# Loading, turning and masking the first batch of an attention and graph-attention kernel in another order

## The chip, the cores and the metric

The kernel runs on one core of a Trainium2 chip. The metric is the device time of one execution in microseconds (us), as the median of repeated runs. Engines are named as in the profile: PE is TensorE (matmul; PEld its weight loads), DVE is VectorE, ACT is ScalarE, POOL is GpSimd, SP is SyncE, which here only issues loads and stores.

## The reference

x is 8 x 2048 x 256, adj is 2048 x 2048. Two layers, each followed by a residual and a layer norm. Layer 0 is attention with 4 heads of 64, in which the softmax is taken separately in each of 8 chunks of 256 keys and the 8 results are added. Layer 1 is graph attention with additive scores.

```python
# layer 0
q, k, v = x @ Wq.T + bq, x @ Wk.T + bk, x @ Wv.T + bv        # then split into heads
scores = clip(q . k / 8, -10, 10)                            # (b, h, n, chunk, key in chunk)
attn = softmax(where(mask == 0, -10, scores))                # over the keys of one chunk
ctx = einsum('bhnjc,bhjcd->bhnd', attn, vc)                  # summed over chunks
y = layernorm(ctx @ Wo.T + bo + x) * gamma + beta
x1 = layernorm(x + y)
# layer 1
Wh = (x1 @ W).reshape(B, N, 4, 64)
e = leaky_relu(s_src[i] + s_dst[j], 0.2), -inf where adj == 0
h = elu(softmax(e, over j) @ Wh)
out = layernorm(x1 + h)
```

## The kernel before

The work goes batch by batch, eight times. Everything on each engine runs in the order in which the program text issues it.

**The head.** `project(b, g)` makes the five steps of group g (512 of the 2048 nodes; four groups): `load` fetches x, `turn` brings features onto the partitions (`xT`), then come keys, values and queries, which are matmuls against `wk_sb` (L315), `wv_sb` (L331) and `wq_sb` (L315) with an evacuation by ACT each (L323, L338). Here `load` is `load_turned`: eight DMAs (L269) of 64 KB in pieces of 32 floats, laid out so that one 32 x 32 block transpose on DVE (L281, `turned`) finishes the turn. For batch 0 this runs alone, before any attention.

**The masks.** `Masks` cuts adj into 48 pieces: 16 tiles of 128 rows times three banks of 6, 5 and 5 column tiles. Each call of `masks.step()` first sends pending stores, then loads one piece (`araw`, L214), turns an earlier one (`turn`: bf16 transposes on PE into `pm`, L236, then DVE writes `clip`, L238, and ACT writes `edge`, L240) and makes the 0/1 bits `ab` of another (L226). The stores go to `clipD`, one table for each quarter of the queries, and `edgeD`, one for each bank. Seventeen steps lie between the pieces of the head; the others are taken one per slot in batch 0.

**Constants.** `finish_constants` folds `a_src` and `a_dst` into `w1_sb` (`wa`, L167 and L168 on DVE), multiplies the value bias through the output weights (L178 on PE) and corrects `bo_sb` and `beta_sb`. It is called after the head. Its `wa` tiles share two buffers with `clip`.

**Slots.** A batch of attention is 64 slots: four query chunks (`q`), two head pairs, eight key chunks, so 16 slots (`i`) for each query chunk. A slot computes the scores of the next slot on PE (L371, `ps`), clips and masks them on DVE against an int8 `slab` loaded from `clipD` (L382, `pr`), exponentiates on ACT (L394) and multiplies by the values on PE (`product`, L406); POOL normalizes and adds up. The work on the chunk finished before (`Between`: output projection L521, two norms, then x1 stored to DRAM and loaded again turned as `x1t`) is spread over slots by the tables AHEAD, BESIDE, BEHIND and AFTER: x1t is loaded in slot 12, DVE turns it in slot 14 (`turn`, L281, `x1T`), and its four layer-1 projections (`values`, L565, `pw`) stand at the ends of slots 14, 15, 0 and 1. In the first chunk's slots there is no such group yet. In slot 61 the first load of the next batch's x is issued, and in slot 63 it is turned on DVE.

**Between batches** an explicit list (`order`) interleaves the last chunk's work with the next batch's keys, values and queries. From batch 1 on, the slots also carry layer 1 of the batch before (L702 on DVE, L722 on PE).

PSUM for projections, scores and wide outputs comes from two tiles of two banks used in turn (`two_banks`); `psM` is one bank, `psL` two.

Of the kernel before, what the change touches and what calls it, by code (L numbers as in the profile page):

```python
# [22 lines left out]
def adj_resnorm_kernel(  # L23
# [19 lines left out]
    nc = tc.nc  # L43
    B, N, F = x.shape
    H, D = a_src.shape
    NT = N // P
    NCH = N // CH
# [8 lines left out]
    QT = CH // P  # L56
    CLIP = 10.0 * 8.0
    FAR = 100.0
    BANKS = (6, 5, 5)
# [139 lines left out]
    class Masks:  # L199
# [1 line left out]


        def __init__(self):
            self.pieces = [(t, m) for t in range(NT) for m in range(len(BANKS))]
            self.raw, self.bits, self.done = [], [], []
            self.next = 0

# [50 lines left out]
    def load_x(b, g, name):  # L258
        t = blocks.tile([P, QT, F], F32, tag="xb", name=name)
        nc.sync.dma_start(out=t, in_=by_node(x, b, g))  # L260
        return t
# [12 lines left out]
    def load_turned(dram, b, g, name):  # L274
        t = blocks.tile([P, KC, CH], F32, tag="xb", name=name)
        load_squares(t, dram[b, g * CH : (g + 1) * CH, :])
        return t

    def turned(t, name):
        dst = blocks.tile([P, KC, CH], F32, tag="xT", name=name)  # L280
        nc.vector.transpose(dst.rearrange("p c n -> p (c n)"), t.rearrange("p c n -> p (c n)"))  # L281
        return dst

    def transposed(src, name):

        dst = blocks.tile([P, KC, CH], F32, tag="xT", name=name)
        pt = two_banks([P, KC, CH], "pt")
        for c in range(KC):
            for k in range(QT):
                nc.tensor.transpose(  # L290
                    pt[:, c, k * P : (k + 1) * P], src[:, k, c * P : (c + 1) * P], identf
                )
        nc.scalar.copy(dst, pt)
        return dst

    def project(b, g):

        cols = slice(g * CH, (g + 1) * CH)
        st = {}

        def load():
            st["x"] = load_turned(x, b, g, "xp")

        def turn():
            st["xT"] = turned(st["x"], "xT")

        def linear(dst, w, bias, apart=False):
            if apart:
                pps = [psL.tile([P, CH], F32, tag="psL", name="pp") for _ in range(KC)]
            else:  # L310
                pp = two_banks([P, KC, CH], "pp")
                pps = [pp[:, c, :] for c in range(KC)]
            for c in range(KC):
                for kc in range(KC):
                    nc.tensor.matmul(  # L315
                        pps[c],
                        lhsT=w[:, kc, c * P : (c + 1) * P],
                        rhs=st["xT"][:, kc, :],
                        start=(kc == 0),
                        stop=(kc == KC - 1),  # L320
                    )
            for c in range(KC):
                nc.scalar.activation(  # L323
                    dst[:, c, cols], pps[c], AF.Identity, bias=bias[:, c : c + 1]
                )

        def values():
            pv = two_banks([P, QT, F], "pv")
            for u in range(QT):
                for kc in range(KC):  # L330
                    nc.tensor.matmul(  # L331
                        pv[:, u, :],
                        lhsT=st["xT"][:, kc, u * P : (u + 1) * P],
                        rhs=wv_sb[:, kc, :],
                        start=(kc == 0),
                        stop=(kc == KC - 1),
                    )
            nc.scalar.copy(  # L338
                vaug[:, QT * g : QT * (g + 1), :, :D],
                pv.rearrange("p t (h d) -> p t h d", h=H),  # L340
            )

        return [
            load,
            turn,
            lambda: linear(kT, wk_sb, bk_sb),
            values,
            lambda: linear(qT, wq_sb, bq_sb, b > 0 and g == NCH - 1),
        ]
# [145 lines left out]
    class Between:  # L495
# [88 lines left out]
    BESIDE = {  # L584
        1: [lambda o: o.bias()],
        4: [lambda o: o.add((0, 1))],
        5: [lambda o: o.add((2, 3)), lambda o: o.a.stats((0, 1))],
        6: [lambda o: o.a.stats((2, 3)), lambda o: o.shift()],
        8: [lambda o: o.scale()],
        9: [lambda o: o.again(), lambda o: o.b2.stats((0, 1))],  # L590
        10: [lambda o: o.b2.stats((2, 3))],
        14: [lambda o: o.turn()],
# [6 lines left out]
        14: lambda o: o.values((0,)),  # L599
        15: lambda o: o.values((1,)),  # L600
    }
    AFTER = {0: lambda o: o.values((2,)), 1: lambda o: o.values((3,))}

    def factors(b, sd, waug):
# [203 lines left out]

    masks = Masks()
    groups = [project(0, g) for g in range(NCH)]  # L810
    groups[0][0]()
    for _ in range(2):
        masks.step()
    groups[1][0]()
    for g in range(NCH):
        for k, piece in enumerate(groups[g][1:]):
            if k == 1 and 0 < g < NCH - 1:
                groups[g + 1][0]()
            piece()
            if g or k:  # L820
                masks.step()
    finish_constants()

# [41 lines left out]
    for b in range(B):  # L867
# [12 lines left out]
        if closing:  # L880
            closing.do(-1)
        group = None
        for s in range(SLOTS):
            q, hp, c = where[s]
            i = s % QS
            send()
            if s + 3 < SLOTS:
                load_slab(s + 3)
            if i == 0:
                before = group  # L890
                group = Between(b, q - 1, sd, waug) if q else None
            if i == 1 and q:
                load_context(b, q - 1, 1)
            if i == QS // 2 + 1:
                load_context(b, q, 0)
            if group and i in AHEAD:
                AHEAD[i](group)
            if s == SLOTS - 3 and b + 1 < B:
                turns = [project(b + 1, g) for g in range(NCH)]
                turns[0].pop(0)()  # L900
            if s:
                normalize(s - 1)
            if s + 1 < SLOTS:
                scores(s + 1)

            if s == SLOTS - 1 and b + 1 < B:
                turns[0].pop(0)()
            if i == 3 and q:
                turn_context(q - 1, 1)
            if i == QS // 2 + 3:  # L910
                turn_context(q, 0)
            if group:
                for step in BESIDE.get(i, ()):
                    step(group)
            elif closing:
                closing.do(s, behind=False)
            product(s, 0, not lower)
            if s + 1 < SLOTS:
                for u in range(KT):
                    exps(s + 1, u)  # L920
            if lower:
                if b + 1 < B or s < SLOTS - LATE:
                    lower.step()
            elif masks.left():
                masks.step()
            product(s, 1, not lower)

            if before and i in AFTER:
                AFTER[i](before)
            if i == 0 and q:  # L930
                send_context(b, q - 1, 1)
            if i == QS // 2:
                send_context(b, q, 0)
            if group and i in BEHIND:
                BEHIND[i](group)
            elif closing and not q:
                closing.do(s, beside=False)
        normalize(SLOTS - 1)
# [2 lines left out]
        before = group  # L941
        gd, fs = factors(b, sd, waug)
        group = None
# [21 lines left out]
        if b + 1 < B:  # L965
            (k0, v0, q0), (l1, t1, k1, v1, q1), (l2, t2, k2, v2, q2), (l3, t3, k3, v3, q3) = turns
            rest = [lambda: lower.rest(1)] if lower else []
            order = [begin, *rest, l1, *rest, lambda: before.values((2, 3)), *rest, ctx, *rest, k0]
            order += [steps[0], t1, steps[1], v0, steps[2], steps[3], l2, k1, steps[4], q0]
            order += [steps[5], v1, t2, l3, steps[6], q1, steps[7], k2, steps[8], steps[9], t3, v2]  # L970
            order += [lambda: [load_slab(s) for s in range(3)], fs[0], q2, fs[1], k3, fs[2], v3]
            order += [lambda: scores(0), q3, lambda: [exps(0, u) for u in range(KT)]]
        else:

            step = lower.step
            order = [begin, lambda: before.values((2, 3)), steps[0], step, ctx, step, steps[1], step]
            order += [steps[2], step, steps[3], step, steps[4], step, steps[5], step, steps[6], step]
            order += [steps[7], step, steps[8], step, steps[9], step, fs[0], step, fs[1], step, fs[2]]
            order += [step, lambda: lower.rest(4)]
            assert sum(p is step for p in order) == LATE  # L980
# [61 lines left out]
```

## Time and profile before

| | us |
|---|---|
| median of 7 runs (range) | 3843.93 (3842.74 to 3847.5) |
| the profiled execution, device time | 3843.94 |
| its span, first to last instruction | 3842.1 |
| PE busy | 3685.4 (96%) |
| DVE busy | 3204.3 (83%) |
| ACT busy | 1948.2 (51%) |
| POOL busy | 1385.4 (36%) |
| first matmul starts | 17.77 |
| last projection of the head ends | about 74.3 |
| first masked scores of slot 0 on DVE | 80.99 |
| keys of batch 1 start | 408.29 |

The granted TensorE clock of the execution is 0.993 of full speed. Matmuls are pipelined and their ends are modelled, so a busy PE is not PE at its peak. Durations are read from one profiled execution, and starts are counted from the start of its span.

### The profile page before, as it was taken

To read this page: it belongs to the slowest core of one execution; us is meant where nothing else is said; L and a number is where in the kernel's file an instruction comes from. 1 tells how busy PE (TensorE), PEld (TensorE's weight loads), DVE (VectorE), ACT (ScalarE), POOL (GpSimd) and SP (SyncE) were. 2 spreads that over 40 slices of the span, in tenths; PEclk is the share of its full clock that TensorE was granted. 3 is DMA by queue.
4 is the path that set the end of the run, shared out by engine and by line. 5 is a ranking of instruction groups with operands and counts; after the bars stand their busy time and mean duration, and the time that the engine had idled before them with its cause. 6 is when DMAs were issued, how large, how long until landed. Compare 5 with 4: busy or idle time off the path is not lost. (4 is left out here: it accounts for less than half of the span.)

```text
span 3842.1 us, 160215 instructions
## 1 busy us (share of the span) xinstructions
PE 3685.4 (96%) x72068; PEld 2745.0 (71%) x72068; DVE 3204.3 (83%) x4810; ACT 1948.2 (51%) x3601; POOL 1385.4 (36%) x1202
## 2 busy tenths in 40 slices
PE   6999999999999999999999999999999999999787
PEld 4656677776777777776777767777677777776676
DVE  3876499986999779995999959998699977998798
ACT  3666445554555555554555545555455555555321
POOL 0444233342343333433443324343343333334310
PEclk9999999999999999999999999999999999999999
DMA  7642333333443343333433334333343433333354
GB/s 149 155 110 62 84 94 99 97 92 100 112 103 99 82 122 103 100 97 82 135 94 100 99 89 136 97 98 88 106 112 97 103 83 116 106 100 85 93 149 123
DMA packets 771328, 398.48 MB, mean 104 GB/s; under 512 B 442576, under 2 KB 735824, under 8 KB 770640
## 3 DMA queue, kind: packets, MB, share of 16 engines
q1 hardware_dynamic: 720640, 354.54, 36.6%
q10 hardware_dynamic: 50000, 33.70, 2.7%
q8 instruction: 563, 9.22, 1.0%
q14 instruction: 125, 1.02, 0.1%
HBM read 331.22 MB, written 56.89 MB: 101 GB/s over the span
## 5 line engine op out<-in xcount | busy, mean ns | idle before, releaser
L382 DVE SCALAR_TENSOR_TENSOR pr<-ps,slab 128x1024 f32<-128x1024 f32 x1024 | 1192.7, 1206 | 213.5 <-PE ps L371 210.8
L702 DVE SCALAR_TENSOR_TENSOR e<-srow,gd,et 128x640 f32<-128x640 f32 (+1 forms) x1536 | 1349.6, 935 | 9.9 <-PE pa L722 5.4
L406 PEld LDWEIGHTS pc<-vaug,pr 128*64 128x64 f32 x32768 | 1040.6, 138 | 440.3 <-issue 257.5
L406 PE MATMUL pc<-vaug,pr 128*64 128x65 f32 x32768 | 1158.2, 224 | 38.8 <-ACT raw L413 31.0
L394 ACT ACTIVATE pr<-pr 128x1024 f32<-128x1024 f32 x1024 | 1049.2, 1057 | 151.3 <-DVE pr L382 137.5
L722 PE MATMUL pa<-waug,e 128*64 128x65 f32 x32768 | 1081.4, 224 | 42.6 <-DVE e L702 40.0
L722 PEld LDWEIGHTS pa<-waug,e 128*64 128x64 f32 x32768 | 1020.0, 139 | 68.2 <-DVE e L702 41.0
L371 PE MATMUL ps<-qT,kT 64*128 64x512 f32 x4096 | 1026.8, 618 | 6.9 <-DVE pr L382 6.6
L428 POOL TENSOR_TENSOR part<-raw,rd 128x512 f32<-128x512 f32 x448 | 468.7, 1046 | 1464.6 <-DVE rd L421 1452.1
L413 ACT COPY raw<-pc 128x260 f32<-128x260 f32 x1024 | 385.0, 377 | 1193.6 <-PE pc L406 1149.6
L371 PEld LDWEIGHTS ps<-qT,kT 64*128 64x128 f32 x4096 | 351.1, 186 | 331.8 <-issue 204.4
L430 POOL TENSOR_TENSOR acc<-acc,part 128x512 f32<-128x512 f32 x448 | 574.1, 1281 | 35.2
L421 DVE RECIPROCAL rd<-raw 128x8 f32<-128x8 f32 x512 | 101.2, 198 | 118.7 <-ACT raw L413 115.2
L428 POOL TENSOR_TENSOR acc<-raw,rd 128x512 f32<-128x512 f32 x64 | 66.7, 1043 | 347.2 <-DVE rd L421 346.4
L750 ACT ACTIVATE hh<-pa,dn 128x64 f32<-128x64 f32 x512 | 114.5, 320 | 100.7 <-DVE dn L746 100.7
L565 PE MATMUL pw<-w_sb,x1T 128*128 128x264 f32 x512 | 138.4, 406 | 7.8 <-DVE x1T L281 7.8
L315 PE MATMUL pp<-xT,wk_sb 128*128 128x512 f32 x256 | 120.1, 613 | 26.4 <-DVE xT L281 19.8
L481 POOL TENSOR_TENSOR rs_c<-rs_c,nhalf 128x4 f32<-128x4 f32 x32 | 55.6, 1737 | 228.7 <-DVE off_c L480 228.7
L521 PE MATMUL po<-wo_sb,qT 128*128 128x256 f32 x512 | 125.5, 390 | 2.1 <-DVE qT L448 1.5
L281 DVE STREAM_TRANSPOSE xT<-xp 128x1024 f32<-128x1024 f32 x32 | 39.6, 1239 | 105.0 <-PE pw L565 67.0
L315 PE MATMUL pp<-xT,wq_sb 128*128 128x512 f32 x256 | 116.1, 596 | 0.0
L331 PE MATMUL pv<-wv_sb,xT 128*128 128x256 f32 x512 | 115.9, 380 | 0.0
(90 smaller groups left out, 1896.6 us busy)
## 6 DMA issues: line engine op xcount, KB each, us to landing
et<-edgeD SPq DMA_DIRECT2D x256, 320.0 KB, 3.2
slab<-clipD SPq DMA_DIRECT2D x512, 128.0 KB, 3.5
et<-edgeD SPq DMA_DIRECT2D x128, 384.0 KB, 3.4
srow<-rowD SPq DMA_DIRECT2D x64, 320.0 KB, 4.3
xp<-in_x_dram SPq DMA_DIRECT2D x256, 64.0 KB, 2.3
xg<-in_x_dram SPq DMA_DIRECT2D x32, 512.0 KB, 4.7
x1D<-y ACTq DMA_DIRECT2D x32, 512.0 KB, 3.1
x1g<-x1D SPq DMA_DIRECT2D x32, 512.0 KB, 5.7
```

Source lines behind the costliest of these rows:

```text
L315: nc.tensor.matmul(pps[c], lhsT=w[:, kc, c * P : (c + 1) * P], rhs=st["xT"][:, kc, :], start=(kc == 0), stop=(kc == KC - 1),)
L371: nc.tensor.matmul(ps[:, k, :], lhsT=kT[rows, hp, t * P : (t + 1) * P], rhs=qT[rows, hp, cols], start=True, stop=True,)
L382: nc.vector.scalar_tensor_tensor(pr, pss[u], -CLIP, slab[:, u, :].unsqueeze(1).to_broadcast([P, 2, CH]), op0=ALU.max, op1=ALU.min,)
L394: nc.scalar.activation(pr, pr, AF.Exp, scale=0.125)
L406: nc.tensor.matmul(pc[z * D : (z + 1) * D, i, :], lhsT=probs[s][u][:, k, i * P + z * D : i * P + (z + 1) * D], rhs=vaug[:, KT * c + u, 2 * ...
L413: nc.scalar.copy(raws[s][:, k], pc)
L428: nc.gpsimd.tensor_mul(part, raw[:, :, :, :D], rd.to_broadcast([P, 2, QT, D]))
L430: nc.gpsimd.tensor_add(accv, accv, part)
L521: nc.tensor.matmul(po[:, k, :], lhsT=qT[:, c, t * P : (t + 1) * P], rhs=wo_sb[:, c, :], start=(c == 0), stop=(c == KC - 1),)
L565: nc.tensor.matmul(pw[:, k, : F + 2 * H], lhsT=self.x1T[:, c, u * P : (u + 1) * P], rhs=w1_sb[:, c, :], start=(c == 0), stop=(c == KC - 1),)
L702: nc.vector.scalar_tensor_tensor(e[:, :w], self.rows[n][:, :w], self.gd[:, h, j : j + 1], self.edge[k // JG][:, j % JG, :w], op0=ALU.max, ...
L722: nc.tensor.matmul(self.pa[z * D : (z + 1) * D, i * D1 : (i + 1) * D1], lhsT=e[:, i * P + z * D : i * P + (z + 1) * D], rhs=self.waug[:, j ...
```

## The change

It touches the head and batch 0 only.

- The 48 mask pieces are taken quarter by quarter and, inside a quarter, bank by bank, where before each row tile went through its three banks. Sizes and number stay.
- In batch 0, x is loaded with one plain DMA for each group (`load_x`) and turned by eight fp32 transposes on PE into a two-bank PSUM tile, which DVE copies to `xT`. Later batches keep the eight strided loads and the block transpose.
- The head's order is written out: loads of groups 0 and 1 first, two mask steps, the turn of group 0; then for each group keys, step, values, step, turn of the next group, load of the one after, queries, step. That is fourteen mask steps in the head; the remaining ones are in slots.
- `finish_constants` is called after the queries of group 1.
- In batch 0, x1's turn moves from slot 14 to 15, and its four projections from the ends of slots 14, 15, 0, 1 to those of 15, 0, 1, 2. For the last chunk the second of them goes into the list between batches.

```diff
@@ class Masks
-            self.pieces = [(t, m) for t in range(NT) for m in range(len(BANKS))]
+            self.pieces = [
+                (QT * q + u, m) for q in range(NCH) for m in range(len(BANKS)) for u in range(QT)
+            ]
@@ transposed, project
-    def transposed(src, name):
+    def transposed(src, name, copy=nc.scalar.copy):
...
-        nc.scalar.copy(dst, pt)
+        copy(dst, pt)
...
         def load():
-            st["x"] = load_turned(x, b, g, "xp")
+            st["x"] = load_turned(x, b, g, "xp") if b else load_x(b, g, "xp")
 
         def turn():
-            st["xT"] = turned(st["x"], "xT")
+            if b:
+                st["xT"] = turned(st["x"], "xT")
+            else:
+                st["xT"] = transposed(st["x"], "xT", nc.vector.tensor_copy)
@@ tables of the slots
+    BESIDE_0 = {i: steps for i, steps in BESIDE.items() if i != 14} | {15: BESIDE[14]}
+    BEHIND_0 = {i: step for i, step in BEHIND.items() if i != 14} | {15: BEHIND[14]}
+    AFTER_0 = {i: lambda o, i=i: o.values((i + 1,)) for i in range(3)}
@@ the head
     groups[0][0]()
+    groups[1][0]()
     for _ in range(2):
         masks.step()
-    groups[1][0]()
+    groups[0][1]()
     for g in range(NCH):
-        for k, piece in enumerate(groups[g][1:]):
-            if k == 1 and 0 < g < NCH - 1:
-                groups[g + 1][0]()
-            piece()
-            if g or k:
-                masks.step()
-    finish_constants()
+        _, _, keys, values, queries = groups[g]
+        keys()
+        masks.step()
+        values()
+        masks.step()
+        if g + 1 < NCH:
+            groups[g + 1][1]()
+        if g + 2 < NCH:
+            groups[g + 2][0]()
+        queries()
+        masks.step()
+        if g == 1:
+            finish_constants()
@@ the slots
+        beside, behind, after = (BESIDE, BEHIND, AFTER) if b else (BESIDE_0, BEHIND_0, AFTER_0)
...
@@ between batches
-            order = [begin, *rest, l1, *rest, lambda: before.values((2, 3)), *rest, ctx, *rest, k0]
+            first = [] if b else [lambda: before.values((1,))]
+            order = [begin, *rest, l1, *rest, *first, lambda: before.values((2, 3))]
+            order += [*rest, ctx, *rest, k0]
```

More of the change, by code (lines that the diff above doesn't have):

```diff
@@ L912, in adj_resnorm_kernel @@
             if group:
-                for step in BESIDE.get(i, ()):
+                for step in beside.get(i, ()):
                     step(group)
@@ L926, in adj_resnorm_kernel @@
             product(s, 1, not lower)
-            if before and i in AFTER:
-                AFTER[i](before)
+            if before and i in after:
+                after[i](before)
             if i == 0 and q:
@@ L933, in adj_resnorm_kernel @@
                 send_context(b, q, 0)
-            if group and i in BEHIND:
-                BEHIND[i](group)
+            if group and i in behind:
+                behind[i](group)
             elif closing and not q:
```

## The prediction

> **What bounds the kernel now.** The page comes first: 3842.1 us of span, PE busy 96%, clock nine tenths or more throughout. Eight batches make that span and the diff touches only the head and batch 0, so the rest was left and the head read in the timeline. All times below are us of the profiled execution.
>
> ```profile
> 16.47 1.25 DVE L281 STREAM_TRANSPOSE xT<-xp 128x1024 f32<-128x1024 f32 x1 [16.47 <-DMA xp<-in_x_dram]
> 17.77 5.09 PE L315 MATMUL pp<-xT,wk_sb 128*128 128x512 f32 x8 [17.77 <-DVE xT L281]
> 45.72 1.24 DVE L281 STREAM_TRANSPOSE xT<-xp 128x1024 f32<-128x1024 f32 x1
> 45.86 0.51 PE L236 MATMUL pm<-identb,ab 128*128 128x128 bf16 x6 [1.39 <-DVE ab L226]
> 47.02 5.40 PE L315 MATMUL pp<-xT,wk_sb 128*128 128x512 f32 x8 [0.64 <-DVE xT L281]
> ```
>
> Columns: start, busy time, what, count, and in brackets the idle time before it and who ended it. TensorE does nothing until 17.77, because SP needs 12.16 to issue eight loads of x. Between groups it waits for the mask bits and then for DVE's transpose.
>
> ```profile
> 74.34 1.08 PE L178 MATMUL pb<-wo_sb,bv_sb 128*128 128x256 f32 x4
> 75.35 1.99 PE L371 MATMUL ps<-qT,kT 64*128 64x512 f32 x8
> 79.40 0.43 DVE L167 TENSOR_TENSOR wa<-w_sb,a_sb 128x256 f32<-128x256 f32 x1 [1.02 <-DMA clipD<-clip]
> 80.99 2.35 DVE L382 SCALAR_TENSOR_TENSOR pr<-ps,slab 128x1024 f32<-128x1024 f32 x2
> 82.26 3.56 PE L371 MATMUL ps<-qT,kT 64*128 64x512 f32 x8 [4.92 <-DVE pr L382]
> ```
>
> The head ends with 6.65 from the last projection (74.34) to the first clipped scores (80.99). The scores are in PSUM by 76.4; finish_constants holds DVE. TensorE idles 4.92 and its next eight score matmuls take 3.56 where 1.99 is usual.
>
> In the windows view (PE busy is the first pair, then PEld, DVE, ACT, POOL, clock, DMA share, GB/s) PE fills the stretch between the gaps:
>
> ```profile
> 47.00:63.00 16.00, 13.84 (x54) 7.86 (x54) 6.37 (x10) 6.44 (x9) 0.00 (x0) 0.89 0.87 168
> 63.00:75.00 12.00, 12.00 (x51) 7.44 (x52) 4.07 (x7) 5.12 (x8) 0.00 (x0) 1.00 0.74 151
> ```
>
> Last, the delayed x1T at two ends of a chunk:
>
> ```profile
> 318.59 1.25 DVE L281 STREAM_TRANSPOSE x1T<-x1t 128x1024 f32<-128x1024 f32 x1 [0.93 <-issue]
> 319.89 1.16 PE L565 MATMUL pw<-w_sb,x1T 128*128 128x264 f32 x4 [2.94 <-DVE x1T L281]
> 401.88 1.25 DVE L281 STREAM_TRANSPOSE xT<-xp 128x1024 f32<-128x1024 f32 x1 [2.95 <-DMA xp<-in_x_dram]
> ```
>
> **The change, part by part.** Minus is time saved.
>
> *1. First x.* One 512 KB load replaces eight. The same shape (xg) lands 3.9 to 6.9 after issue, median 4.7; it competes with the weights here (wk_sb 4.2, the last row load 6.7), so I take 6.2: issue 0.73, landed 6.9. Eight fp32 transposes follow. In batch 0's end five of L290 take 0.77 warm, so eight take 1.2; from idle I double that, by L315's 1222 ns cold against 592 warm: 2.4. DVE's copy out of PSUM is not in the trace; L382 reads PSUM at the same size in 1.21, ACT's L293 copies it in 1.01; I take 1.2. Keys of group 0 then start at 10.5 instead of 17.77: -7.2. Ends: landed at 4.6 and all warm gives 6.9 (-10.9); x landing only with everything issued beside it, 2.2 MB at the 245 GB/s of the first loads, 11.0, gives 14.7 (-3.1).
> The first matmul stretch is taken cold as before (5.09 against 3.70). The Trainium skill ("TensorE: Matmul & The Clock Gate", Part 4) says transposes do not count as activity for the clock; by that the 5.09 stays, and if they do count the sum is 1.4 lower. No row here decides it.
> Added wait: eight completion semaphores take turns, so ACT's late constant loads now wait for x and the first two adjacency loads, and ACT's first evacuation is queued behind them. Those 1.8 MB with 1.3 MB of weights should be in by about 15 at that rate, and keys end at 15.6, with the PSUM buffer wanted at 19.5: costed at nothing, one for one beyond about 18.
>
> *2. Groups.* Before, keys of groups 0, 1, 2, 3 begin at 17.77, 32.89, 47.02, 62.91 and the last queries end at 74.34: 15.1, 14.1, 15.9, 11.4. Group 3 has no gaps: 11.4 is PE work with three mask turns. After, the turn is issued before the preceding queries, so 3.65 of matmul cover the 1.2 copy; each of groups 0 to 2 carries 1.2 of transposes. Group 0: 11.4 + 1.4 cold - 0.45 (only two mask turns) + 1.2 = 13.6. Group 1: 11.4 + 1.2 + the moved L178 1.08 = 13.7. Group 2: 12.6. Group 3: 11.4. Together 51.3 against 56.6: -5.2 (-3.5 if group 2's slow keys, 5.40 for 3.70, come again). Queries end at 61.8.
> If the queries did not cover the copy, each group would pay its 1.2. On SP each load of x now stands between a mask's load and the next stores; its buffer was read by the turn two groups earlier, so it waits for nothing late.
> finish_constants on DVE now lies behind group 1, under keys and values of group 2 (7.6). Its DVE work is 4.2 (four pairs of 0.43 and 0.42, then 0.41 and 0.42), but it shares the clip buffers and waits for stores of clip that reach SP only about then (landing 1.9 to 4.3): +0.5, ends 0 and +3. Behind it queue clip and ab of the next mask, for which PE's turn waits.
>
> *3. To the first clipped scores.* DVE is free, so the slab decides: before, it was issued at 73.63, 3.06 after queries began (70.57), and the slabs of this stretch land in 3.9. Queries begin at 58.0, the slab is in at 65.0, 3.2 after the end: 6.65 becomes 3.2, -3.5. Ends: scores ready first (76.4 less 74.34, and L178 gone from between), -5.0; slab in 7.5, the slowest of the run, 0. PE's idle shrinks to about 1.3: 80.99 to the third pair at 90.24 is 9.25; the pair's 2.35 and one usual slot of 4.51 would be 7: -1.0 (0 to -2).
>
> *4. Masks.* Seventeen mask steps in the head become fourteen; three move to slots. A slot has 4.51 between pairs with a mask, 3.91 without: +1.8. Ends: 0.6 to 1.8 each (the slow slots near 200). Bank order alters neither sizes nor counts, and every slab's pieces are stored before its load is issued: nothing.
>
> *5. x1T a slot later.* The four L565 steps go along, to slots 15, 0, 1 and 2, the same matmuls and ACT copies; psM is free again before L521 needs it in slot 3, and the load stays in slot 12. Chunk 1: no DMA wait at 237.97, so the 2 us of PE idle just move. Chunk 2: the 0.93 wait goes, -0.9. Chunk 3: x1T now stands on DVE behind xT of the next batch, which waits for x until 401.88. So x1T ends at 404.4. PE, idle from about 400, then does all sixteen pw (twelve took 2.94, so 3.9, plus 0.8 for ACT to clear the single psM buffer) until 409.1, where before they ended at 406.5. The context's transposes then waited for POOL; keys began at 408.29 and will near 409.8: +1.5 (0 to +3.5).
>
> Sum: -7.2 -5.2 +0.5 -3.5 -1.0 +1.8 -0.9 +1.5 = -14.0. The profiled execution took 3843.94 (the span and 1.84 around it), the median of the seven runs is 3843.93: 3829.9.
>
> **The rivals.** *Late x* (0.11): the first load shares its engines evenly with all that is issued beside it; part 1 gives 3.1, sum -9.9, 3834.0. For it: DMA share 0.77 in the first 17. Against: xg's slowest row, 6.9.
> *Swallowed* (0.09): DVE waits for clip stores (+3 for 0.5), the slab comes late (0 for -3.5), slow keys return (+1.7): 7.7 less gain, 3837.6. For it: DMA share 0.97 from 33 to 47. Against: of all L382 pairs one waited for a slab, 0.4, and the small x loads leave that stretch.
> *Cold clock* (0.05), the slower one: with transposes and copies between the projections TensorE stays at its slow clock in the head. A wholly cold group costs 11.0 x 1.06 = 11.7 more, so from 1.2 cold groups on nothing is left; two give 3853.3, which is slower by over 0.2%, three 3865. For it: the 0.89 above, after waits of 1.39 and 0.64. Against: the clock of 1.00 from 63 to 75 with mask transposes between projections, and the waits being taken away.
> That the order does not change as said is ruled out by the changed program's instruction order.
>
> **How the numbers follow.** Forecast 0.75, late x 0.11, swallowed 0.09, cold clock 0.05. Within 0.2% (7.7, about what this measurement can tell from no change) lies only swallowed: 0.09; faster is forecast and late x, 0.86; slower 0.05. The range: the favourable ends of parts 1 and 3 together with a clean part 5 reach -20.7; with late and favourable ends unlikely at once I stop at 3824. Above, late x and swallowed: 3838.
>
> **What would show it.** Keys of group 0 near 10.5; gaps under 0.5 before keys of groups 1 to 3; queries ending near 62; first L382 pair near 65, its wait ended by a slab; third pair near 73; 37 mask turns in slots; x1T of chunk 2 without a DMA wait; keys of batch 1 some 13 to 15 earlier than 408.29. It is wrong if keys of group 0 start after 15, if the clock from 17 on in the head falls under 0.9, or if batches 1 to 7 change length.

## The result and the profile after

The changed kernel's median is 3832.06 us over 13 runs (3827.8 to 3836.12), against 3843.93 us for the kernel before over 33 runs (3839.99 to 3847.5). The ratio is 0.9969 [0.9962, 0.9977]: 11.9 us are gained where 14.0 had been forecast. The profiled execution took 3832.15, with a span of 3830.4 against 3842.1. The clock granted over the whole span is the same (0.992 against 0.993). The DMA moves the same 398.5 MB in 756545 packets instead of 771328.

The timeline of the head after the change comes first (start, busy time, what, count, and in brackets the idle time before it and who ended it):

```profile
5.88 1.94 PE L292 MATMUL pt<-identf,xp 128*128 128x128 f32 x8 [5.88 <-DMA xp<-in_x_dram]
...
7.86 1.23 DVE L295 COPY xT<-pt 128x1024 f32<-128x1024 f32 x1 [7.86 <-PE pt L292]
...
9.14 6.34 PE L321 MATMUL pp<-xT,wk_sb 128*128 128x512 f32 x8 [1.32 <-DVE xT L295]
...
31.58 1.04 PE L292 MATMUL pt<-identf,xp 128*128 128x128 f32 x8
...
32.52 3.70 PE L321 MATMUL pp<-xT,wq_sb 128*128 128x512 f32 x8
...
33.05 1.22 DVE L295 COPY xT<-pt 128x1024 f32<-128x1024 f32 x1
...
37.25 3.60 PE L321 MATMUL pp<-xT,wk_sb 128*128 128x512 f32 x8
```

The first keys start at 9.14 instead of 17.77. From then on the turn of a group has no bracket: its transposes follow other matmuls without a gap, the copy on DVE (33.05 to 34.27) lies wholly inside the queries (32.52 to 36.22), and the next keys find `xT` ready. The windows view of the stretch in which the kernel before had its gaps (width, then busy time and instructions of PE, PEld, DVE, ACT and POOL, then clock, DMA share, GB/s):

```profile
33.00:47.00 14.00, 14.00 (x62) 8.81 (x61) 9.63 (x19) 6.16 (x9) 0.00 (x0) 1.00 0.69 157
47.00:63.00 16.00, 15.98 (x66) 8.54 (x64) 5.21 (x9) 7.33 (x11) 0.00 (x0) 1.00 0.70 147
```

PE is full and the granted clock is at 1.00, as it is from 17 to 33. Before, the second of these windows had 13.84 of PE at 0.89. The head ends so:

```profile
60.97 2.28 PE L377 MATMUL ps<-qT,kT 64*128 64x512 f32 x8
...
63.55 4.81 DVE L388 SCALAR_TENSOR_TENSOR pr<-ps,slab 128x1024 f32<-128x1024 f32 x4 [1.24 <-DMA slab<-clipD]
...
64.83 2.26 PE L377 MATMUL ps<-qT,kT 64*128 64x512 f32 x8 [1.58 <-DVE pr L388]
...
71.51 2.32 DVE L388 SCALAR_TENSOR_TENSOR pr<-ps,slab 128x1024 f32<-128x1024 f32 x2
```

The first clipped scores come at 63.55 instead of 80.99. A slab decides them now (1.24 of wait), and TensorE idles 1.58 there instead of 4.92. The third pair of clipped scores, slot 2, starts at 71.51 instead of 90.24: up to there 18.7 are gained. Last, the delayed x1T, at chunk 1 and at the end of the batch:

```profile
227.25 2.13 PE L571 MATMUL pw<-w_sb,x1T 128*128 128x264 f32 x4 [2.47 <-DVE x1T L283]
...
229.31 3.77 PE L377 MATMUL ps<-qT,kT 64*128 64x512 f32 x8
...
384.70 1.25 DVE L283 STREAM_TRANSPOSE xT<-xp 128x1024 f32<-128x1024 f32 x1 [3.94 <-DMA xp<-in_x_dram]
385.87 1.20 DVE L283 STREAM_TRANSPOSE x1T<-x1t 128x1024 f32<-128x1024 f32 x1
...
387.13 2.12 PE L571 MATMUL pw<-w_sb,x1T 128*128 128x264 f32 x4 [4.91 <-DVE x1T L283]
...
389.79 4.69 PE L571 MATMUL pw<-w_sb,x1T 128*128 128x264 f32 x12 [0.54 <-ACT sd L582]
```

In the kernel before, the same two places read:

```profile
239.26 2.13 PE L565 MATMUL pw<-w_sb,x1T 128*128 128x264 f32 x4 [1.98 <-DVE x1T L281]
...
241.32 2.54 PE L371 MATMUL ps<-qT,kT 64*128 64x512 f32 x8
...
403.57 2.94 PE L565 MATMUL pw<-w_sb,x1T 128*128 128x264 f32 x12
```

At chunk 1 the scores behind the first `pw` take 3.77 where they took 2.54 before and 1.99 is usual. At the end of the batch x1T stands behind xT, which waits 3.94 for x; PE waits 4.91 for x1T, and twelve `pw` take 4.69 instead of 2.94.

A ledger read from the starts of the clipped scores shows where the rest went. "2 to 31" is the time from the pair of slot 2 to that of slot 31, and so on; the last chunk's end runs from slot 63 to the first clipped scores of batch 1 (slot 62 to 63 takes 3.91 in every kernel).

| us | pair of slot 2 | 2 to 31 | 31 to 36 | 36 to 46 | 46 to 52 | 52 to 62 | 63 to batch 1 | first pair of batch 1 |
|---|---|---|---|---|---|---|---|---|
| before | 90.24 | 145.48 | 28.81 | 46.88 | 32.24 | 46.87 | 63.60 | 458.03 |
| after | 71.51 | 145.57 | 31.85 | 47.81 | 28.69 | 47.43 | 67.73 | 444.50 |
| x1T in slot 14 again (first profile) | 70.99 | 145.56 | 27.83 | 47.08 | 32.23 | 46.91 | 65.48 | 439.99 |
| x1T in slot 14 again (second profile) | 71.42 | 145.48 | 27.83 | 47.07 | 32.05 | 46.88 | 62.99 | 437.63 |
| x1T ahead of xT in slot 63 | 71.59 | 145.56 | 31.20 | 47.79 | 30.34 | 47.43 | 62.56 | 440.39 |
| later turn in chunk 2 alone | 70.47 | 145.50 | 29.47 | 47.07 | 28.69 | 47.41 | 64.41 | 436.93 |

Of the 18.7 gained, 5.2 are given back between slot 2 and batch 1: 3.0 at chunk 1 (31 to 36), 0.9 and 0.6 in the slots after chunks 1 and 2, and 4.1 at the end of the batch, with 3.5 gained at chunk 2 (46 to 52). A further 1.7 go in batches 1 to 7, whose program is the same.

### The profile page after: what moved, and what is told of

It is laid out like the page before. It is cut to its first block, busy times and chain, and to the rows that moved or that the text cites. A ratio compares the mean times of both kernels' runs of the same rounds, so it can differ in the third digit from the quotient of the medians.

```text
span 3830.4 us, 160246 instructions
## 1 busy us (share of the span) xinstructions
PE 3691.1 (96%) x72100; PEld 2752.2 (72%) x72100; DVE 3203.6 (84%) x4810; ACT 1950.1 (51%) x3601; POOL 1384.7 (36%) x1202
## 2 busy tenths in 40 slices
DMA packets 756545, 398.50 MB, mean 104 GB/s; under 512 B 425744, under 2 KB 721040, under 8 KB 755856
## 5 line engine op out<-in xcount | busy, mean ns | idle before, releaser
L434 POOL TENSOR_TENSOR acc<-raw,rd 128x512 f32<-128x512 f32 x64 | 66.8, 1043 | 333.6 <-DVE rd L427 332.8
L571 PEld LDWEIGHTS pw<-w_sb,x1T 128*128 128x128 f32 x512 | 92.8, 194 | 32.4 <-DVE x1T L283 10.9
```

What stands on the lines that cost most here:

```text
L434: nc.gpsimd.tensor_mul(part, raw[:, :, :, :D], rd.to_broadcast([P, 2, QT, D]))
L571: nc.tensor.matmul(pw[:, k, : F + 2 * H], lhsT=self.x1T[:, c, u * P : (u + 1) * P], rhs=w1_sb[:, c, :], start=(c == 0), stop=(c == KC - 1),)
```

## The experiments

The kernels were timed in three series of four, in the order of the table and each on another chip, with the kernel before beside them every time (3843.51, 3843.79 and 3844.31). "Gain" is that median less the kernel's own. The edits are against the changed kernel unless it is said otherwise.

| kernel | median us | ratio to the kernel before | gain |
|---|---|---|---|
| x1T in slot 14 again | 3826.27 | 0.9955 [0.9941, 0.9968] | 17.2 |
| x1T later, last chunk left | 3827.96 | 0.9961 [0.9948, 0.9973] | 15.6 |
| x1T ahead of xT in slot 63 | 3827.17 | 0.9958 [0.9945, 0.997] | 16.3 |
| seventeen mask steps | 3840.76 | 0.9992 [0.9983, 1.0001] | 2.8 |
| the changed kernel | 3830.91 | 0.9963 [0.9949, 0.9977] | 12.9 |
| constants after the head | 3834.84 | 0.9975 [0.9965, 0.9984] | 9.0 |
| masks in row order | 3830.34 | 0.9963 [0.995, 0.9975] | 13.5 |
| kernel before, plain load alone | 3834.45 | 0.9975 [0.9965, 0.9986] | 9.3 |
| strided load in the new order | 3836.73 | 0.998 [0.9972, 0.9989] | 7.6 |
| later turn in chunk 2 alone | 3823.95 | 0.995 [0.9936, 0.9963] | 20.4 |
| chunks 2 and 3, x1T first | 3823.64 | 0.9949 [0.9936, 0.9961] | 20.7 |
| x1T in slot 14 again, second time | 3823.74 | 0.9949 [0.9937, 0.9962] | 20.6 |

One and the same kernel gained 17.2 in the first series and 20.6 in the third, so differences across series are read to some 3 us and no closer. Inside a series, too, most of these medians are of five runs that lie 4 to 6 us apart, so a difference of 2 us between two of them is not clear of the noise.

**The changed kernel again** is the yardstick of the second series.

> The changed kernel as it is, beside the next three on the same chip: 3832 within 2 us, 11 to 13 under the kernel before. Rival: it is really near 3828 and its distance to the three versions that move x1's turn in batch 0 differently (3826.3 to 3828.0) is chance.

Measured: 12.9, with the pair of slot 2 at 72.25 and batch 1's first pair at 445.26. The gain is confirmed (11.9 in the first runs), and the rival, a time near 3828, is not borne out.

**x1T back in slot 14.** All three tables are those of the later batches.

```diff
-        beside, behind, after = (BESIDE, BEHIND, AFTER) if b else (BESIDE_0, BEHIND_0, AFTER_0)
+        beside, behind, after = BESIDE, BEHIND, AFTER
...
-            first = [] if b else [lambda: before.values((1,))]
+            first = []
```

> The changed kernel, with x1's turn and its four projections back in their places of before (slots 14, 15, 0, 1). By the two traces' ledger the move saved 3.8 us in chunk 2 (no load wait and no slow clock after it) and lost 4.1 at the end of batch 0 (x1T queued behind xT), so undoing it gives the changed kernel's time within 1 us, about 3832, with keys of batch 1 at 394 to 395; the stall returns in chunk 2 and the 4.9 us of PE idle in slot 63 goes. The prediction's own part 5 (+0.6 for the move) gives 3831.5. Rival: the loss at the batch's end has another cause than the move; then undoing it only loses chunk 2's gain, 3836, with keys of batch 1 at 398.

Measured: 3826.27, a gain of 17.2. The end of the batch, in the timeline of this kernel:

```profile
377.06 1.25 DVE L283 STREAM_TRANSPOSE x1T<-x1t 128x1024 f32<-128x1024 f32 x1 [0.21 <-DMA x1t<-x1D]
...
378.36 1.47 PE L571 MATMUL pw<-w_sb,x1T 128*128 128x264 f32 x4 [2.23 <-DVE x1T L283]
...
383.02 2.94 PE L571 MATMUL pw<-w_sb,x1T 128*128 128x264 f32 x12
```

PE waits 2.23 for x1T instead of 4.91, its twelve `pw` take 2.94 instead of 4.69, and they start at 383.02 instead of 389.79. Of that 6.8, the head's own difference is 0.5, and 1.7 come from the slots between. Neither expected time came: the undone kernel is 5 to 6 us faster than the two that were named for it (3832 and 3831.5). The same kernel once more, in the third series:

> The version with all turns of x1 in slot 14 once more, as the measure for the three beside it: 17 under the kernel before, 3826.5 within 2. Rival: its lead of 4.5 over the changed kernel was chance; then 3830.

Measured: 3823.74, a gain of 20.6 and 2.8 less time than expected. Without the later turn the change is worth 17.2 and 20.6; with it 11.9 and 12.9. Over all ten and all eighteen runs the medians are 3825.8 and 3831.5: the move of x1T costs 5.7.

**x1T later, but not in the last chunk.**

```diff
+        after = AFTER if b else AFTER_0
...
+            late = b == 0 and q < NCH - 1
+            beside, behind = (BESIDE_0, BEHIND_0) if late else (BESIDE, BEHIND)
...
-            first = [] if b else [lambda: before.values((1,))]
+            first = []
```

> The changed kernel, with the last chunk of batch 0 alone back to slots 14 and 15 as before; chunks 1 and 2 keep the later turn. If the last chunk's x1T behind xT is what lost 4.1 us, this keeps chunk 2's 3.8 and drops the loss: about 3828, keys of batch 1 near 391. Rival: the end of the batch waits for the next batch's x in either order, so that an earlier slot 63 is only waited away: at most 1 us better, keys at 394.

Measured: 3827.96 as expected, a gain of 15.6, 1.7 short of the full undoing in the same series, which is within the noise. In the ledger of its profile "63 to batch 1" is 64.45, against 67.73 in the changed kernel: most of the loss is the last chunk's. The timeline at chunk 1 shows a second thing:

```profile
225.39 1.16 PE L571 MATMUL pw<-w_sb,x1T 128*128 128x264 f32 x4 [2.47 <-DVE x1T L283]
...
226.47 1.99 PE L377 MATMUL ps<-qT,kT 64*128 64x512 f32 x8
```

The idle time is the 2.47 of the changed kernel, yet the matmuls behind it run at their usual 1.16 and 1.99, where they took 2.13 and 3.77 above. The windows view tells the two apart (the changed kernel, then this one; the third number from the end is the granted clock):

```profile
226.00:233.00 7.00, 5.75 (x12) 2.36 (x12) 3.73 (x6) 2.48 (x6) 2.64 (x3) 0.51 0.62 160
225.00:232.00 7.00, 6.61 (x85) 4.35 (x85) 5.18 (x8) 3.95 (x9) 2.32 (x2) 1.00 0.65 179
```

Behind the same gap TensorE was granted half its clock in the one execution and all of it in the other.

**x1T ahead of xT in slot 63.** All of the later turn stays, but DVE turns x1 before the next batch's x.

```diff
-            if s == SLOTS - 1 and b + 1 < B:
+            if s == SLOTS - 1 and 0 < b and b + 1 < B:
                 turns[0].pop(0)()
...
+                if s == SLOTS - 1 and b == 0:
+                    turns[0].pop(0)()
```

> The changed kernel, with one exchange on DVE in slot 63 of batch 0: x1T is issued before xT of the next batch. x1t has landed by then, so x1T should run near 381, the projections of x1 from 382 instead of 387 and at a warm clock, and keys of batch 1 near 391: about 3828.5. Rival: xT's wait for its load (until 384.7) and the context's transposes behind POOL decide when keys start; then keys start at 393 or later and the time is that of the changed kernel within 1.5 us.

Measured: 3827.17, close to what was expected, a gain of 16.3. The timeline at the batch's end:

```profile
382.01 1.25 DVE L283 STREAM_TRANSPOSE x1T<-x1t 128x1024 f32<-128x1024 f32 x1 [0.19 <-DMA xp<-in_x_dram]
...
385.00 2.94 PE L571 MATMUL pw<-w_sb,x1T 128*128 128x264 f32 x12 [0.54 <-ACT sd L582]
385.37 1.25 DVE L283 STREAM_TRANSPOSE xT<-xp 128x1024 f32<-128x1024 f32 x1 [2.12 <-DMA xp<-in_x_dram]
```

x1T no longer stands behind the wait for x, the twelve `pw` are back at 2.94, and "63 to batch 1" is 62.56, against 67.73 in the changed kernel and 63.60 before. The same instructions in another order on DVE remove the loss: that x1T was held up by the waiting xT is shown.

**Later turn where it should help.** Chunk 2 alone:

```diff
+        LATE_Q = (2,) if b == 0 else ()
...
+            beside, behind = (BESIDE_0, BEHIND_0) if q in LATE_Q else (BESIDE, BEHIND)
+            after = AFTER_0 if q - 1 in LATE_Q else AFTER
```

> The changed kernel with the later turn of x1 in chunk 2 alone; chunks 1 and 3 turn in slot 14 as before. By the ledger of stretches slot 15 costs 1.6 in chunk 1, saves 1.9 to 3.5 in chunk 2 (less 0.5 in the slots behind) and costs 3.9 at the end of the batch: so 2 to 3 less than with all turns in slot 14 (3826.3 when measured), about 3824. Rival: chunk 2's stall of the old place does not return once the head has moved everything; then no difference to it, within 1.

And chunks 2 and 3 (`LATE_Q = (2, 3)`), with x1T ahead of xT in slot 63:

> The changed kernel with chunk 1's turn back in slot 14, chunks 2 and 3 in slot 15, and x1T issued on DVE before xT of the next batch in slot 63. By the ledger the end of the batch then takes 62.6 from the last pair to the next batch's first, against 63.7 with the turn in slot 14: about 3823.5. Rival: the saving at the end is eaten by the slots before it (the projections in slots 0 to 2); then as the version with chunk 2 alone, within 1.

Measured: 3823.95 and 3823.64, beside 3823.74 without any later turn. In the ledger "46 to 52" is 28.69 in the one and 30.33 in the other, against 32.05 for the undone kernel, so something is gained there; at the level of whole runs the three can't be told apart. Both times came out as expected, but so would the rivals' have, and the lead over the undone kernel that was expected is not there: these runs don't decide. They are the fastest kernels of this study, 20.4 to 20.7 under the kernel before.

**Constants late**, as in the kernel before:

```diff
-        if g == 1:
-            finish_constants()
+    finish_constants()
```

> The changed kernel with finish_constants after the head again. DVE is free at 62.3 in the changed kernel and would then need 4.2 to 5.2 for the constants, so the first masked scores come at 67 to 68 instead of 63.55, PE idles some 5 us and the next scores are slow: 4 to 5.5 us more, about 3837. L178 leaves the place behind group 1 (1.08) and returns behind the head. Rival: the constants cost as much under group 2 by delaying the masks there, so that the place does not matter: within 1 us of the changed kernel.

Measured: 3834.84 against 3830.91 in the same series, so the early place is worth 3.9, where 4 to 5.5 were expected. Timeline of this kernel:

```profile
63.84 0.43 DVE L167 TENSOR_TENSOR wa<-w_sb,a_sb 128x256 f32<-128x256 f32 x1 [0.72 <-DMA clipD<-clip]
...
65.42 2.35 DVE L388 SCALAR_TENSOR_TENSOR pr<-ps,slab 128x1024 f32<-128x1024 f32 x2
...
66.69 3.79 PE L377 MATMUL ps<-qT,kT 64*128 64x512 f32 x8 [4.62 <-DVE pr L388]
```

The picture of the kernel before is back: `wa` waits for a clip store, PE idles 4.62 before the next scores and runs them in 3.79. The first pair is 2.4 later than in the changed kernel of the same series (63.06) and the third pair 2.9 later (75.14 against 72.25).

**Mask pieces in row order.**

```diff
-            self.pieces = [
-                (QT * q + u, m) for q in range(NCH) for m in range(len(BANKS)) for u in range(QT)
-            ]
+            self.pieces = [(t, m) for t in range(NT) for m in range(len(BANKS))]
```

> The changed kernel with the mask pieces in row order again, all else kept. The prediction gave the order nothing: the changed kernel's time within 1 us. Rival: with only fourteen steps in the head the piece that the first slab needs (fourth row tile, first bank) is then the tenth and not the fourth, stored just before the slab is loaded; the slab waits for that store to land (2.4), the first masked scores come 1 to 3 us later than 63.55 and PE's idle time grows: 1 to 4 us more.

Measured: 3830.34 against 3830.91. The bank order makes no difference that can be seen.

**Seventeen mask steps in the head.**

```diff
         masks.step()
+        if g:
+            masks.step()
         if g == 1:
             finish_constants()
```

> The changed kernel with 17 mask steps in the head instead of 14 (one more after the queries of groups 1, 2 and 3), so three fewer in slots. The prediction's term: a mask in a slot costs 0.6 us, a turn on PE in the head 0.45; then the time falls by only 0.5 us (3831.5), and the first masked scores come 1.4 later than 63.55. Rival: the 4 us that the changed kernel loses against the one before between the pairs of slots 31 and 46 are the three masks, 1.3 each; then it falls by 2.6 to about 3829.5.

Measured: 3840.76, a gain of only 2.8. Both expected times, 3831.5 and 3829.5, are missed by far, and the timeline says why:

```profile
51.46 0.45 PE L238 MATMUL pm<-identb,ab 128*128 128x128 bf16 x5 [1.32 <-DVE ab L228]
...
66.56 1.28 SPq L364 DMA_DIRECT2D slab<-clipD  x3
...
70.48 2.36 DVE L388 SCALAR_TENSOR_TENSOR pr<-ps,slab 128x1024 f32<-128x1024 f32 x2 [3.70 <-DMA slab<-clipD]
```

Two steps with no projection between them leave PE waiting for the bits (1.32 here and at the group before, 1.52 at the last). The first slab is issued on SP at 66.56, where the changed kernel issues it at 59.91, and DVE waits 3.70 for it. The pair of slot 2 comes at 80.76. So this kernel's time measures two new waits and not the masks' share in the slots. That share can be read from single slots: the last mask turn comes in slot 34 here and in slot 37 of the changed kernel, and slots 35 to 37, from pair to pair, take 17.05 here and 18.34 there. Three masks in slots cost 1.3.

**The plain load alone**, on the kernel before, with its order of the head kept:

```diff
-            st["x"] = load_turned(x, b, g, "xp")
+            st["x"] = load_turned(x, b, g, "xp") if b else load_x(b, g, "xp")
...
-            st["xT"] = turned(st["x"], "xT")
+            if b:
+                st["xT"] = turned(st["x"], "xT")
+            else:
+                st["xT"] = transposed(st["x"], "xT", nc.vector.tensor_copy)
```

> The kernel before with one part of the change alone: plain loads of x, turned on PE and copied by DVE, in the old order, with the old masks, constants and x1 turn. By the ledger the first keys start near 9.2 instead of 17.77 (8.6 gained); but the turn now stands on PE just before the keys that need it, so in groups 1 to 3 PE waits for its 1.04 and for DVE's copy behind clip and ab: about 1 more than the old gap each, 3 in all. Net 5 to 6 gained, 3838. Rival: the gap is the same as with DVE's transpose, and the whole 8.6 stays: 3835.

Measured: 3834.45, a gain of 9.3. Its timeline has the first keys at 9.20, and in front of the next group:

```profile
24.63 3.67 PE L318 MATMUL pp<-xT,wk_sb 128*128 128x512 f32 x8 [0.77 <-DVE xT L293]
```

Without the new order the copy is not covered, but it costs only 0.77, 0.71 and 0.77 at the three later groups. In return the waits of 1.32 to 1.45 for mask bits, which the kernel before has in front of each of these groups, shrink to 0.44 to 0.57. So the rival came true, and the whole gain of the first load stays.

**All but the plain load**: strided loads and block transposes in the new order.

```diff
-            st["x"] = load_turned(x, b, g, "xp") if b else load_x(b, g, "xp")
+            st["x"] = load_turned(x, b, g, "xp")
...
-            if b:
-                st["xT"] = turned(st["x"], "xT")
-            else:
-                st["xT"] = transposed(st["x"], "xT", nc.vector.tensor_copy)
+            st["xT"] = turned(st["x"], "xT")
```

> The changed kernel with the eight strided loads and DVE's block transpose in batch 0 again, in the new order of the head. Against the changed kernel the first keys should start 8.6 later (near 17.8), and PE is rid of its transposes (four times 1.04): the head ends some 4.5 later, first masked scores near 68, about 3836. With the kernel that has the plain load alone (9.3 gained of 12.4) this tells whether the two parts add up. Rival: sixteen strided loads ahead of the first masks on SP hold the masks back as well; then PE waits for ab in groups 0 and 1 and the first masked scores come after 71, 3839 or more.

Measured: 3836.73, close to the expected 3836, a gain of 7.6. First keys:

```profile
16.60 5.40 PE L318 MATMUL pp<-xT,wk_sb 128*128 128x512 f32 x8 [16.60 <-DVE xT L283]
```

They start 7.5 later than with the plain load (9.14), but the pair of slot 2, at 77.84, is only 6.3 later than in the changed kernel, and the gain 5.3 smaller than the 12.9 of the second series. The eight transposes of 1.04 in each of three groups, and 1.94 in the first, are PE time that the block transposes on DVE don't need. The load alone (9.3) and all the rest (7.6) add up to 16.9, more than the 11.9 to 12.9 of both together: each removes a part of the same waits. Of the three waits of PE for mask bits between the groups (1.32, 1.39 and 1.45 before), 0.44 to 0.57 each are left with the load alone, and a single one of 0.84 in this kernel.

## Why the prediction was right, and where its terms were off

The time, 3832.06, lies in the range and 2.2 above the forecast. Two errors, of opposite sign, stand behind that: parts 1 to 3 gave 18.7 where they had 16.4, and parts 4 and 5 with the batches after them took 6.9 (18.7 less the 11.8 between the two profiled executions) where they had 2.4. The head's mechanism was right; that the sum came out so close is in part luck.

*Part 1, -7.2 for the first x: -8.6.* The load landed by 5.88, where 6.9 was taken. The cold transposes took 1.94 for 2.4 and the copy 1.23 for 1.2. The keys then ran cold, as taken (1.22 for the first matmul and 1.06 for each of the next five, where 0.59 is usual), but in 6.34 instead of 5.09; in the other profiles with this load they took 5.26 to 6.33, and with the strided loads in the new order, where no transposes stand ahead of them, 5.40. The eight transposes ahead did not make them fast, so the 1.4 that would have come off if transposes counted did not. The Trainium skill ("TensorE: Matmul & The Clock Gate", Part 4) says that the full clock doesn't engage for transposes; this trace agrees, with the reserve that 1.32 of idle time lies between them and the keys. The added wait on ACT cost nothing, as costed: ACT evacuates the first keys at 15.52, waiting for PE. The rival of a late x is out with the load's landing.

*Part 2, -5.2 for the groups and +0.5 for the constants.* Groups 0 to 2, from keys to keys, took 14.77, 13.34 and 12.31 where 13.6, 13.7 and 12.6 were taken; from the first keys to the first scores (60.97) it is 51.8 for 51.3. The 1.2 too much in group 0 is the longer cold stretch. The constants now stand on DVE between 37.67 and about 42, and no idle time of PE stands there: 0 for the +0.5. The rival of a cold clock is out by the granted clock of 1.00 from 17 to 63 and the 3.60 to 3.70 of every eight projections there, that of the swallowed gain by this and by the first pair.

*Part 3, -3.5 and -1.0.* The first pair came at 63.55 for 65, its wait ended by a slab as said, and PE's idle time was 1.58 for 1.3. The late constants measure the two terms by themselves: 3.9 in medians and 2.9 at the third pair, for 4.5.

*Part 4, +1.8 for three mask steps in slots: +0.9 to +1.3.* This term was mis-sized. In the sum from slot 2 to batch 1 nothing of it is seen: 369.0 and 366.2 in the two profiles with fourteen steps and x1T in slot 14, against 367.8 before and 368.0 with the plain load alone. But these sums move by some 3 us with the granted clock at the ends of chunks, and single slots show it. Slots 35 to 37, which have masks only with fourteen steps in the head, take 16.53 in both kernels with seventeen steps and the old turn of x1 in chunk 1, and 17.42 in all four profiles with fourteen; with the later turn they take 17.05 with seventeen steps and, in all seven profiles with fourteen, 18.3 to 18.4. "A slot has 4.51 between pairs with a mask, 3.91 without" is a true reading, but the difference was charged in full to each moved step; 0.3 to 0.4 a step arrived. The bank order cost nothing that can be seen, as said.

*Part 5, +0.6 net for x1T a slot later: +3.6 to +5.7.* This is the step that failed, and three of its readings were off. The means are over all profiles with and without the move at each place. In all of them the `pw` and scores at chunks 1 and 2 ran long exactly where the trace has the granted clock at half, and at their usual 1.16 and 1.99 where it has 1.00.

- Chunk 1, "the 2 us of PE idle just move": they grew from 1.98 to 2.47. "31 to 36" is 30.5 over eight profiles with the move (28.4 to 31.9) and 28.8 over six without (27.8 to 29.7), and "36 to 46" 0.7 longer: +2.3. Where the clock stayed at 1.00, "31 to 36" took 27.83 with the old turn (both profiles of the undone kernel) and 28.36 with the later one: only 0.5 of the 1.6 comes with the clock at its full, the rest is mostly how often it fell.
- Chunk 2, "the 0.93 wait goes, -0.9": the wait goes, but so does, in six of ten profiles, a slow stretch behind it. PE's gap there is 1.90 instead of 2.94, and its `pw` and scores ran at full speed in the changed kernel:

```profile
308.10 1.16 PE L571 MATMUL pw<-w_sb,x1T 128*128 128x264 f32 x4 [1.90 <-DVE x1T L283]
...
309.19 1.99 PE L377 MATMUL ps<-qT,kT 64*128 64x512 f32 x8
```

 "46 to 52" is 28.7 to 30.3 in ten profiles with the move and 32.1 to 32.2 in four without: -2.8, with +0.4 in the slots after it.
- Chunk 3, +1.5: the mechanism was right (x1T behind a waiting xT, sixteen `pw` then in a row), but the sixteen were priced warm, 3.9. After 4.91 of idle they took 2.12 and 4.69, 6.8, with a granted clock of 0.51 from 386.5 to 393.5. "63 to batch 1" is 67.7 over six profiles (66.8 to 68.9) and 64.0 over six with the old turn: +3.7, just over the end that was given for it.

Together +3.6 by these means, which take in kernels that differ in other things too. The two kernels that differ in this move alone, with two profiles each, take 373.0 twice and 369.0 and 366.2 from slot 2 to batch 1: +5.4, close to the 5.7 between their medians.

*Batches 1 to 7* were assumed to keep their length. From the first pair of batch 1 to the end of the span it is 3384.11 before and 3385.85 after, but over the fourteen profiles, all with this same program there, the figure runs from 3383.6 to 3386.6. One profile can't tell 1.7 from no change, and it stays open whether any of it is real.

## What to carry to other kernels

On an engine that works in order, moving a step later moves it behind whatever was queued in between: look first whether that instruction waits for a transfer, and if so put the moved one ahead of it (here some 4 us at the end of the batch, 67.7 to the 62.56 and 64.16 of the two kernels with the lines swapped). Price what comes after an idle TensorE at the durations of half its clock too, and let matmuls that are ready cover the copies that bring the next operand. When two edits remove waits at the same place, measure each alone, since their gains don't add.

## What the runs showed of the hardware that was not expected

- The same gap does not always cost the same, and the granted clock tells the cases apart. After 2.47 of idle TensorE at chunk 1, the four `pw` and eight scores took 1.16 and 1.99 in one kernel, 2.13 and 2.51 in a second profile of the changed kernel, and 2.13 and 3.77 in its first: 3.2 to 5.9 for the same twelve instructions. After 1.98 the kernel before took 2.13 and 2.54 (granted clock 0.51 from 239.0 to 242.5), and the undone one 1.16 and 1.99 (1.00 from 218 to 225). What decides whether the clock falls after such a gap is not shown. A single profile therefore gives one of several prices for a gap. The Trainium skill ("TensorE: Matmul & The Clock Gate", "Why this matters for your kernels") asks for no idle gaps over about 3 us; here slow matmuls followed gaps of 1.9 to 2.5 as well.
- Eight fp32 transposes of 128 x 128 take 1.04 among other matmuls and 1.94 from idle, and DVE's copy of 128 x 1024 fp32 out of PSUM 1.22.
- With the clock at 1.00 from 17 to 63, transposes between the projections did not slow the projections: 3.60 to 3.70 for each eight matmuls.
